# A graph layer on one core: two engines copy a tile of rows in every eighth chunk instead of every sixteenth

## The chip, the cores and the metric

The kernel runs on one core of a Trainium2 chip. The metric is the device time of one execution in microseconds; the median over several runs counts. The core has five engines that each work through a queue of instructions in order: TensorE (PE in the profile, its weight loads PEld), VectorE (DVE), ScalarE (ACT), GpSimd (POOL) and SyncE (SP). SP does nothing but issue transfers; ACT and POOL issue transfers beside their own work. Engines wait for each other, and for transfers, by semaphores.

## The reference, cut to what matters

50000 nodes have 128 features each; 850000 edges (50000 of them loops) have a source, a destination and one of 16 types. A layer adds, for every edge, the source's features times the matrix of the edge's type to the destination, adds the node's own product, and applies relu. There are two such layers; at the end the input is added and each row is normalised.

```python
W = jnp.einsum('rb,bio->rio', w_comp, basis)
seg = dst * N_REL + rel
agg = jax.ops.segment_sum(h[src], seg, num_segments=N_ENT * N_REL)
msg = jnp.einsum('nri,rio->no', agg.reshape(N_ENT, N_REL, -1), W)
h = relu(msg + h @ loop_w + bias)           # twice, with two sets of weights
x = layernorm(x + h)
```

## The kernel before, in words

Each type's matrix is a mix of 8 basis matrices. So the kernel first sums, for each node, its sources' features weighted with each of the 8 coefficients, and multiplies by the 8 basis matrices afterwards, in groups of 512 nodes.

The edges come sorted by destination, with the loops taken out: 800000 of them, in 6250 tiles of 128 edges. Ten tiles (K) make a chunk; there are 625 chunks (C), and a chunk covers about 80 destination nodes. For every tile, 128 rows of features are fetched, one row to a partition, and TensorE multiplies the fetched tile with a matrix `hot` that VectorE makes (the 8 coefficients of every edge at the place of its destination in a window of 30 nodes). VectorE adds the products into a ring in SBUF (lines 1130 on), and a group of 512 nodes that is complete is copied out of the ring by ScalarE (line 915), multiplied by the basis (919), passed through relu (934), turned back and stored.

Nearly all the fetching is done by GpSimd: one indirect transfer for each tile, issued by `gather` (line 270), with the 128 row numbers in a tile `index` that is cast from a packed list for 16 chunks at a time (`indexed`, line 1053). The fetched chunks lie in 4 buffers in the first layer and in 9 in the second; in the order of the program, GpSimd is 2 and 7 chunks ahead of TensorE (FETCH).

A few tiles are fetched in another way. In every sixteenth chunk from EARLY on, tile 9 of the chunk (COPIED) is copied row by row by SP, and in every sixteenth chunk eight chunks apart by ACT: class `Copied`, lines 1172 to 1201. GpSimd skips that tile (line 1250), and TensorE reads the copied tile instead (line 1271). For each such tile `load` (line 1178) fetches 128 offsets from a list AWAY in DRAM into the first partition of the tile itself; `copy` (line 1183) reads sixteen of them into registers (lines 1188 and 1190), takes one (`snap`, line 1191) and issues a transfer of one row of 512 bytes (line 1192). The row of partition 0, where the offsets lie, is copied last. Each of the two copiers has one buffer, and its transfers carry semaphores that the framework deals out in turn from a small set, which SP's and ACT's other transfers use too: a transfer whose semaphore is still owed by an earlier one waits for that.

The order of the work is written out: `later(time, what)` puts a piece of work into a heap by its due time, counted in tiles (10 to a chunk), and the loop over the chunks, which writes TensorE's matmuls, takes from the heap what is due. Rows fall due one by one, evenly over 12 chunks, the last 1.6 chunks ahead of the chunk that needs them (`planned`, line 1197). SP's queue also carries the loads and stores of the groups, of the weights, and of the places in the ring (`offsets`, line 1154); ACT's queue also carries copies and activations. In the first layer the edges of later chunks are prepared along the way (runs, rows_of), with transfers on SP and work on VectorE and ACT.

Of the kernel before, what the change touches and what calls it, by code (L numbers as in the profile page):

```python
# [51 lines left out]
P = 128  # L52
# [4 lines left out]
K = 10  # L57
# [10 lines left out]
PER = 5  # L68
# [4 lines left out]
GATHERS = 4  # L73
J = 4
AHEAD = 16
EACH = 2 * len(WINDOWS)
NEAR = 128
BATCH = 4
# [9 lines left out]
WIDE = 1  # L88
PARTS_OF = ((0, 3), (3, 5))
EPS = 1e-5  # L90
EVERY = 16
COPIED = 9
EARLY = ((27, 35), (19, 27))
LEAD = 2
AT_A_TIME = 16


def divisor(n, most):
# [4 lines left out]
def tile_rgcn_resnorm(  # L103
# [15 lines left out]
    nc = tc.nc  # L119
    N, D = x.shape  # L120
# [3 lines left out]
    C = -(-M // (K * P))  # L124
# [34 lines left out]
    consts = ctx.enter_context(tc.tile_pool(name="consts", bufs=1))  # L159
    col = consts.tile([P, P], F32, name="col")  # L160
    nc.gpsimd.iota(col, pattern=[[1, P]], base=0, channel_multiplier=0, allow_small_or_imprecise_dtypes=True)
    part = consts.tile([P, 1], F32, name="part")
    nc.gpsimd.iota(part, pattern=[[0, 1]], base=0, channel_multiplier=1, allow_small_or_imprecise_dtypes=True)
    ident = consts.tile([P, P], F32, name="ident")
    nc.vector.tensor_scalar(ident, col, part, None, op0=OP.is_equal)

    single = consts.tile([P, 4], F32, name="single")
    eps, apart_by, odd, ones = (single[:, i : i + 1] for i in range(4))
    nc.vector.memset(eps, EPS)

# [12 lines left out]
    def weighed(brief):  # L183


        steps = brief.tile([P, AT - 1], F32, name="steps")
        nc.gpsimd.iota(
            steps, pattern=[[NR, AT - 1]], base=NR, channel_multiplier=0, allow_small_or_imprecise_dtypes=True
        )
        passed = brief.tile([P, AT - 1], F32, name="passed")  # L190
        nc.vector.tensor_scalar(passed, steps, part, None, op0=OP.is_le)
        its_tile = brief.tile([P, 1], F32, name="its_tile")
        nc.vector.tensor_reduce(its_tile, passed, AX.X, OP.add)
        nc.vector.scalar_tensor_tensor(its, its_tile, float(-NR), part, op0=OP.mult, op1=OP.add)
        nc.vector.tensor_scalar(its1, its, 1.0, None, op0=OP.add)
        one_tile = brief.tile([P, AT], F32, name="one_tile")
        nc.vector.tensor_scalar(one_tile, col[:, :AT], its_tile, None, op0=OP.is_equal)
        which = brief.tile([P, PARTS], F32, name="which")
        nc.vector.tensor_scalar(which, col[:, :PARTS], its_tile, None, op0=OP.is_equal)
        again = brief.tile([P, PARTS], F32, name="again")  # L200
        nc.vector.tensor_scalar(again, col[:, PARTS : 2 * PARTS], its_tile, None, op0=OP.is_equal)
        nc.vector.tensor_add(which, which, again)
        for n, (basis, w_comp, loop_w, bias) in enumerate(GIVEN):
            ec = brief.tile([P, NB], F32, name="ec")
            nc.scalar.dma_start(
                ec, bass.AP(tensor=w_comp.tensor, offset=w_comp.offset, ap=[[0, AT], [NB, NR], [1, NB]])
            )
            nc.vector.tensor_tensor(
                each[:, n],
                ec[:, None, :].to_broadcast([P, AT, NB]),  # L210
                one_tile[:, :, None].to_broadcast([P, AT, NB]),
                op=OP.mult,
            )

            column_of = consts.tile([P, 1], F32, name=f"bias_of{n}")
            nc.scalar.dma_start(column_of, bass.AP(tensor=bias.tensor, offset=bias.offset, ap=[[1, P], [1, 1]]))
            BIAS_OF.append(column_of)
            left, mine = ec, brief.tile([P, NB], F32, name="mine")
            for i in range(PARTS):
                short = brief.tile([P, NB], BF16, name=f"short{i}")  # L220
                nc.vector.tensor_copy(short, left)
                if i == 0:
                    nc.vector.tensor_scalar(mine, short, which[:, i : i + 1], None, op0=OP.mult)
                else:
                    nc.vector.scalar_tensor_tensor(
                        mine, short, which[:, i : i + 1], mine, op0=OP.mult, op1=OP.add
                    )
# [333 lines left out]
    def rows_of(j, pool):  # L561
# [12 lines left out]
        keyf, srcf = pair(pool, "real_both", LIVE, LIVE, F32)  # L574
# [6 lines left out]
        def put(of, to):  # L581
# [17 lines left out]
        away = pool.tile([P, LIVE, 2], F32, name="full").bitcast(I32).rearrange("p e w -> p (e w)")[:, :P]  # L599
        of_copied = (COPIED - PER) * P  # L600
        nc.vector.tensor_scalar(
            away[:m], srcf[:m, of_copied : of_copied + P], float(N - 1), float(D), op0=OP.min, op1=OP.mult
        )
        nc.sync.dma_start(AWAY[r0 : r0 + m], away[:m])
        begin = pool.tile([P, len(WINDOWS)], F32, name="begin")
# [110 lines left out]
    def chunked():  # L716
        with (
# [334 lines left out]

            def indexed(n, b, copy):
                first_of, end_of = b * AHEAD * K, min(C, (b + 1) * AHEAD) * K
                index[n, b] = hp.tile([P, AHEAD * K], I32, name="index", bufs=3)
                return copy(index[n, b][:, : end_of - first_of], src[:, first_of:end_of])

            placed = indexed(0, 0, nc.vector.tensor_copy)
# [14 lines left out]
            def later_rows():  # L1073
# [12 lines left out]

            coming = later_rows()
            copiers = [
                (engine, [engine.alloc_register(f"copied{who}_{i}") for i in range(AT_A_TIME)])
                for who, engine in enumerate((nc.sync, nc.scalar))  # L1090
            ]
            ordered = ExitStack()
# [1 line left out]
            for n, of in enumerate((x, H1)):  # L1094
# [19 lines left out]
                def places(c):  # L1114
                    loaded_for[0] = n, c // BATCH
                    some = min(BATCH, C - c) * EACH
                    which_of = c % AHEAD // BATCH * BATCH * EACH
                    nc.vector.load(at_reg[:some], offs[c // AHEAD][0:1, which_of : which_of + some])

                def add(c, half, i, pa):  # L1120

# [30 lines left out]
                offs = {}  # L1152

                def offsets(b):
                    first_of, end_of = b * AHEAD * EACH, min(C, (b + 1) * AHEAD) * EACH
                    offs[b] = hp.tile([1, AHEAD * EACH], I32, name="offs")
# [10 lines left out]
                def go_on(now):  # L1167
                    while events and events[0][0] <= now:
                        _, _, what, args = heapq.heappop(events)
                        what(*args)  # L1170

                class Copied:
                    def __init__(self, c, who):
                        self.c, self.who = c, who
                        self.engine, self.at = copiers[who]
                        self.order = [*range(1, P), 0]

                    def load(self):
                        self.to = hp.tile([P, D], F32, name=f"copied{self.who}", bufs=1)
                        self.away = self.to.bitcast(I32)[0:1, :]  # L1180
                        nc.sync.dma_start(self.away, AWAY[2 * self.c + 1 : 2 * self.c + 2])

                    def copy(self, i):
                        p = self.order[i]
                        if i % AT_A_TIME == 0:
                            some = self.order[i : i + AT_A_TIME]
                            if some[-1] == 0:
                                self.engine.load(self.at[AT_A_TIME - 1 :], self.away[:, 0:1])
                                some = some[:-1]
                            self.engine.load(self.at[: len(some)], self.away[:, some[0] : some[-1] + 1])  # L1190
                        at = self.engine.snap(self.at[i % AT_A_TIME], min_val=0, max_val=(N - 1) * D)
                        self.engine.dma_start(
                            self.to[p : p + 1, :],
                            of.rearrange("n d -> (n d)")[ds(at, D)].rearrange("(o d) -> o d", o=1),
                        )

                    def planned(self, queue):
                        begin = K * (self.c - EVERY + LEAD) + PER
                        queue(begin - K, self.load)
                        for i in range(P):  # L1200
                            queue(begin + i * (EVERY - 2 * LEAD) * K // P, self.copy, i)

                copied_rows = {
                    c: Copied(c, who) for who, early in enumerate(EARLY[n]) for c in range(early, C, EVERY)
# [4 lines left out]
                batches = [Weights(c, n) for c in range(0, C, BATCH)]  # L1209
                batches[0].load()  # L1210
                offsets(0)
                for b in range(1, -(-C // AHEAD)):
                    later(K * AHEAD * b - K, offsets, b)
                if n == 0:
                    batches[0].compare()
                    batches[0].multiply()
# [21 lines left out]
                for c in range(C):  # L1238
# [19 lines left out]
                    for half in range(2):  # L1258
# [6 lines left out]
                        for at in range(PER):  # L1265
                            if at < len(tiles):
# [2 lines left out]
                                w, before = WINDOWS[i], NB * sum(WINDOWS[:i])  # L1269
                                fetched = g[:, half * PER + j, :]  # L1270
                                if half * PER + j == COPIED and c in copied_rows:
                                    fetched = copied_rows[c].to
                                nc.tensor.matmul(  # L1273
                                    pa[:, before : before + NB * w],
                                    fetched,
# [234 lines left out]
```

## Time and profile before

| | |
|---|---|
| runs | 15531.8 us median of 3 (15528.1 to 15533.5) |
| profiled execution | 15567.6 us, its span 15565.8 us |
| busy, PE / DVE / ACT / POOL | 62% / 50% / 11% / 75% of the span |
| TensorE clock granted | 0.794 |
| moved by DMA | 1531 MB, 98 GB/s |
| tiles fetched by GpSimd / by SP and ACT | 12349 / 151 |

The profile is of one execution and its engines are abbreviated as above; a q behind an engine's name means its sequencer, which issues transfers and waits. "L270" is line 270 of the kernel. In groups of instructions, the columns are line, engine, operation, output and input, count, then busy us and mean ns of one, then the idle time of the engine before them and what ended it ("issue" is idle time in which nothing that the profile shows was waited for). Lists of waits give the waiting engine and instruction, what it waited for, the total in us, how often and the longest. Issuing a transfer, register work and waiting don't count as busy.

### The profile page before, as it was taken

How to read it: one execution, taken by the hardware profiler on the slowest of the kernel's cores; microseconds unless marked ns; L12 is line 12 of the kernel's file. 1: busy time of each engine (PE TensorE's matmuls, PEld its weight loads, DVE VectorE, ACT ScalarE, POOL GpSimd, SP SyncE). 2: the span in 40 equal slices, each digit the busy share in tenths (PEclk: the TensorE clock that was granted, in tenths of full speed). 3: DMA queues.
4: the chain of work that ended last, by engine and by line, in shares of the span. 5: the costliest groups of instructions: out<-in, count | busy, mean ns of one | idle time of the engine just before them, and what ended most of it. 6: DMA issues, size and time to landing. Idle time of an engine off the chain costs nothing.

```text
span 15565.8 us, 164019 instructions
## 1 busy us (share of the span) xinstructions
PE 9727.8 (62%) x31567; PEld 7176.4 (46%) x31567; DVE 7738.2 (50%) x11079; ACT 1642.8 (11%) x2031; POOL 11742.7 (75%) x12390
## 2 busy tenths in 40 slices
PE   5666566666666666666666666666666666666666
PEld 4444444444444444444444444444444444444444
DVE  7655555565444444444444444444444444444444
ACT  1111111111111111111100000000000000000000
POOL 7777777777777777777777777777777777777777
PEclk7877887777888888888877777787777777777778
DMA  4333333333333333333333333333333333333332
GB/s 125 109 111 107 109 110 106 107 106 105 99 99 96 99 99 98 98 99 98 94 92 94 94 94 94 93 92 93 94 94 94 94 94 94 92 94 94 94 94 81
DMA packets 827507, 1530.93 MB, mean 98 GB/s; under 512 B 245150, under 2 KB 332937, under 8 KB 826472
## 3 DMA queue, kind: packets, MB, share of 16 engines
q0 software_dynamic: 397104, 817.16, 18.8%
q1 hardware_dynamic: 408424, 697.64, 13.4%
q10 hardware_dynamic: 20944, 5.55, 0.2%
q14 instruction: 778, 6.37, 0.1%
q8 instruction: 257, 4.21, 0.1%
HBM read 1391.28 MB, written 128.09 MB: 98 GB/s over the span
## 4 chain that ended last, share of the span: by engine, by line
POOL 61%; issue 24%; DMA 11%; PE 2%; DVE 1%; SPq 1%; ACTq 0%; ACT 0%; POOLq 0%; DVEq 0%
POOL g L270 43%; DMA g<-in_x_dram,index 5%; POOL d_r L270 4%; POOL k_loop L270 4%; POOL parts L270 4%; POOL full L270 4%; POOL real_both L270 3%; DMA g<-H,index 2%; PE pa L1273 1%; DMA real_both<-H,index 1%; DMA full<-H,index 1%; DMA k_loop<-H,index 1%; DMA parts<-H,index 1%; DMA d_r<-H,index 1%; SPq L1190 0%
## 5 line engine op out<-in xcount | busy, mean ns | idle before, releaser
L1273 PE MATMUL pa<-hot,g 128*128 128x240 f32 x17882 | 5490.0, 459 | 4012.8 <-DMA g<-in_x_dram,index 2195.9
L270 POOL DMA_INDIRECT g<-in_x_dram,index x6175 | 5875.3, 951 | 1890.1 <-issue 1783.7
L1273 PEld LDWEIGHTS pa<-hot,g 128*128 128x128 f32 x17882 | 4155.0, 242 | 5580.4 <-issue 2374.8
L1130 DVE TENSOR_TENSOR ring<-pa,ring 128x240 f32 x5000 | 2038.6, 408 | 7077.2 <-PE pa L1273 6275.3
L1106 DVE TENSOR_TENSOR hot<-pm,fixed 128x2400 f32<-128x2400 f32 x1250 | 3317.9, 2654 | 69.7 <-ACT pm L789 17.4
L270 POOL DMA_INDIRECT g<-H,index x2766 | 2616.6, 946 | 857.1 <-issue 814.1
L919 PE MATMUL pn<-own,basis 128*128 128x512 f32 x3072 | 1808.1, 674 | 0.0
L900 DVE TENSOR_TENSOR ring<-wide,pa 128x2048 f32<-128x2048 f32 (+1 forms) x386 | 876.4, 2270 | 230.8 <-DMA wide<-CW 212.2
L915 ACT COPY own<-ring 128x4096 f32<-128x4096 f32 x192 | 692.3, 3606 | 2444.1 <-DVE ring L1130 1100.6
L270 POOL DMA_INDIRECT k_loop<-H,index x682 | 645.2, 946 | 208.1 <-issue 197.4
L270 POOL DMA_INDIRECT real_both<-H,index x682 | 645.3, 946 | 208.0 <-issue 194.3
L270 POOL DMA_INDIRECT d_r<-H,index x682 | 645.2, 946 | 208.0 <-issue 198.6
L270 POOL DMA_INDIRECT parts<-H,index x681 | 644.3, 946 | 207.8 <-issue 197.4
L270 POOL DMA_INDIRECT full<-H,index x681 | 644.2, 946 | 207.8 <-issue 194.7
L919 PEld LDWEIGHTS pn<-own,basis 128*128 128x128 f32 x3072 | 667.3, 219 | 65.5
L1273 PE MATMUL pa<-hot,real_both 128*128 128x240 f32 x1364 | 445.4, 482 | 334.7 <-DMA real_both<-H,index 317.0
L1273 PE MATMUL pa<-hot,k_loop 128*128 128x240 f32 x1364 | 442.6, 479 | 318.7 <-DMA k_loop<-H,index 287.3
L1273 PE MATMUL pa<-hot,full 128*128 128x240 f32 x1362 | 444.3, 481 | 310.5 <-DMA full<-H,index 292.3
L1273 PE MATMUL pa<-hot,d_r 128*128 128x240 f32 x1364 | 442.6, 479 | 311.7 <-DMA d_r<-H,index 275.2
L1273 PE MATMUL pa<-hot,parts 128*128 128x240 f32 x1362 | 444.4, 481 | 304.1 <-DMA parts<-H,index 268.6
L887 ACT COPY pa<-hT 128x512 f32<-128x512 f32 x392 | 228.8, 587 | 3534.0 <-DMA copied<-H 1798.0
L1099 DVE TENSOR_TENSOR fixed<-fixed,key 128x300 f32<-128x300 f32 x1250 | 584.5, 468 | 1.6
(181 smaller groups left out, 5255.8 us busy)
## 6 DMA issues: line engine op xcount, KB each, us to landing
wide<-CW SPq DMA_DIRECT2D x388, 1024.0 KB
g<-in_x_dram,index POOLq DMA_INDIRECT x6175
copied<-in_x_dram SPq DMA_DIRECT2D x4864, 0.5 KB
copied<-H SPq DMA_DIRECT2D x4864, 0.5 KB
copied<-H ACTq DMA_DIRECT2D x4864, 0.5 KB
copied<-in_x_dram ACTq DMA_DIRECT2D x4736, 0.5 KB
rows<-in_x_dram SPq DMA_DIRECT2D x194, 256.0 KB
g<-H,index POOLq DMA_INDIRECT x2766
```

What stands on the lines that cost most here:

```text
L270: return nc.gpsimd.indirect_dma_start(out=to, out_offset=None, in_=of, in_offset=bass.IndirectOffsetOnAxis(ap=idx, axis=0))
L887: nc.scalar.copy(self.laid[b][:, : self.cnt], self.hT[:, : self.cnt])
L900: nc.vector.tensor_tensor(into, wide, laid[:, None, :].to_broadcast([P, AT_ONCE, cnt]), op=OP.mult)
L915: nc.scalar.copy(self.sums, ring[:, :, at : at + cnt])
L919: nc.tensor.matmul(self.pn[:, a:e], BASIS[:, b, :], self.sums[:, b, a:e], start=False, stop=b == NB - 1)
L1099: nc.vector.tensor_tensor(own, grid[:, None, :].to_broadcast([P, K, WN]), key[:, c * K : (c + 1) * K, None].to_broadcast([P, K, WN]), op=O ...
L1106: nc.vector.tensor_tensor(hot, pm[:, c % BATCH * K * NB : (c % BATCH + 1) * K * NB].rearrange("e (k b) -> e k b", b=NB)[:, :, :, None].to_ ...
L1130: nc.vector.tensor_tensor(into, pa[:, before : before + NB * w].rearrange("d (b w) -> d b w", w=w), into, op=OP.add,)
L1273: nc.tensor.matmul(pa[:, before : before + NB * w], fetched, hot[:, half * PER + j].rearrange("e b w -> e (b w)"), start=(i, j) == mine[i][0],
```

## The change

The copiers take a tile in every eighth chunk each. The due times move: a tile's rows are spread over 8 chunks, and the last is due 0.6 chunk ahead of its chunk. Each copier has two buffers and four semaphores of its own, one for a tile in turn; the rows carry that semaphore and no other, and TensorE waits for it before it reads the tile. The offsets in AWAY are kept in bytes, the rows are addressed as bytes, and the register is used without `snap`. The offsets lie in the last partition of the tile, so rows go in the order 0 to 127. To make room in SBUF, `index` has two buffers and not three, the places in the ring are fetched for 8 chunks at a time, two chunks ahead (they were fetched for 16, one ahead), and some single columns share a tile.

```diff
+PLACED = 8
-EVERY = 16
+EVERY = 8
 COPIED = 9
-EARLY = ((27, 35), (19, 27))
+EARLY = ((20, 24), (12, 16))
 LEAD = 2
 AT_A_TIME = 16
+SIGNALS = 4
+DONE = 16
...
-            away[:m], srcf[:m, of_copied : of_copied + P], float(N - 1), float(D), op0=OP.min, op1=OP.mult
+            away[:m], srcf[:m, of_copied : of_copied + P], float(N - 1), float(4 * D), op0=OP.min, op1=OP.mult
...
-                index[n, b] = hp.tile([P, AHEAD * K], I32, name="index", bufs=3)
+                index[n, b] = hp.tile([P, AHEAD * K], I32, name="index")
...
-                (engine, [engine.alloc_register(f"copied{who}_{i}") for i in range(AT_A_TIME)])
+                (
+                    engine,
+                    [engine.alloc_register(f"copied{who}_{i}") for i in range(AT_A_TIME)],
+                    [tc.alloc_semaphore(f"rows{who}_{i}") for i in range(SIGNALS)],
+                    [0],
+                )
...
-                    which_of = c % AHEAD // BATCH * BATCH * EACH
-                    nc.vector.load(at_reg[:some], offs[c // AHEAD][0:1, which_of : which_of + some])
+                    which_of = c % PLACED // BATCH * BATCH * EACH
+                    nc.vector.load(at_reg[:some], offs[c // PLACED][0:1, which_of : which_of + some])
...
+                bytes_of = of.rearrange("n d -> (n d)").bitcast(U8)
+
                 class Copied:
                     def __init__(self, c, who):
                         self.c, self.who = c, who
-                        self.engine, self.at = copiers[who]
-                        self.order = [*range(1, P), 0]
+                        self.engine, self.at, signals, used = copiers[who]
+                        self.signal = signals[used[0] % SIGNALS]
+                        self.after = (used[0] // SIGNALS + 1) * P * DONE
+                        used[0] += 1
+                        self.group = f"copied{n}_{c}"
 
                     def load(self):
-                        self.to = hp.tile([P, D], F32, name=f"copied{self.who}", bufs=1)
-                        self.away = self.to.bitcast(I32)[0:1, :]
+                        self.to = hp.tile([P, D], F32, name=f"copied{self.who}")
+                        self.away = self.to.bitcast(I32)[P - 1 : P, :]
+                        self.rows = self.to.bitcast(U8)
                         nc.sync.dma_start(self.away, AWAY[2 * self.c + 1 : 2 * self.c + 2])
 
-                    def copy(self, i):
-                        p = self.order[i]
-                        if i % AT_A_TIME == 0:
-                            some = self.order[i : i + AT_A_TIME]
-                            if some[-1] == 0:
-                                self.engine.load(self.at[AT_A_TIME - 1 :], self.away[:, 0:1])
-                                some = some[:-1]
-                            self.engine.load(self.at[: len(some)], self.away[:, some[0] : some[-1] + 1])
-                        at = self.engine.snap(self.at[i % AT_A_TIME], min_val=0, max_val=(N - 1) * D)
-                        self.engine.dma_start(
-                            self.to[p : p + 1, :],
-                            of.rearrange("n d -> (n d)")[ds(at, D)].rearrange("(o d) -> o d", o=1),
+                    def copy(self, p):
+                        if p % AT_A_TIME == 0:
+                            self.engine.load(self.at, self.away[:, p : p + AT_A_TIME])
+                        at = RuntimeValue.of_register_unchecked(
+                            self.at[p % AT_A_TIME], min_val=0, max_val=(N - 1) * 4 * D
                         )
+                        row = self.engine.dma_start(
+                            self.rows[p : p + 1, :], bytes_of[ds(at, 4 * D)].rearrange("(o d) -> o d", o=1)
+                        )
+                        row.then_inc(self.signal, DONE)
+                        tc.no_tile_sem_insts.add(row.ins.name)
+                        tc.add_to_no_dep_group(self.group, row.ins)
+
+                    def landed(self):
+                        tc.declare_fence(nc.tensor.wait_ge(self.signal, self.after).ins, group=self.group)
+                        return self.to
 
                     def planned(self, queue):
-                        begin = K * (self.c - EVERY + LEAD) + PER
+                        begin = K * (self.c - EVERY - LEAD + 1) + PER
                         queue(begin - K, self.load)
                         for i in range(P):
-                            queue(begin + i * (EVERY - 2 * LEAD) * K // P, self.copy, i)
+                            queue(begin + i * EVERY * K // P, self.copy, i)
...
-                for b in range(1, -(-C // AHEAD)):
-                    later(K * AHEAD * b - K, offsets, b)
+                for b in range(1, -(-C // PLACED)):
+                    later(K * PLACED * b - 2 * K, offsets, b)
...
-                                    fetched = copied_rows[c].to
+                                    fetched = copied_rows[c].landed()
```

More of the change, by code (lines that the diff above doesn't have):

```diff
@@ L38 @@
 from concourse._compat import with_exitstack
-from concourse.bass import ds
+from concourse.bass import RuntimeValue, ds
 F32 = mybir.dt.float32
@@ L161, in tile_rgcn_resnorm @@
     nc.gpsimd.iota(col, pattern=[[1, P]], base=0, channel_multiplier=0, allow_small_or_imprecise_dtypes=True)
-    part = consts.tile([P, 1], F32, name="part")
+    single = consts.tile([P, 8], F32, name="single")
+    part = single[:, 4:5]
     nc.gpsimd.iota(part, pattern=[[0, 1]], base=0, channel_multiplier=1, allow_small_or_imprecise_dtypes=True)
@@ L165, in tile_rgcn_resnorm @@
     nc.vector.tensor_scalar(ident, col, part, None, op0=OP.is_equal)
-    single = consts.tile([P, 4], F32, name="single")
     eps, apart_by, odd, ones = (single[:, i : i + 1] for i in range(4))
@@ L213, in weighed @@
             )
-            column_of = consts.tile([P, 1], F32, name=f"bias_of{n}")
+            column_of = single[:, 5 + n : 6 + n]
             nc.scalar.dma_start(column_of, bass.AP(tensor=bias.tensor, offset=bias.offset, ap=[[1, P], [1, 1]]))
@@ L1154, in offsets @@
                 def offsets(b):
-                    first_of, end_of = b * AHEAD * EACH, min(C, (b + 1) * AHEAD) * EACH
-                    offs[b] = hp.tile([1, AHEAD * EACH], I32, name="offs")
+                    first_of, end_of = b * PLACED * EACH, min(C, (b + 1) * PLACED) * EACH
+                    offs[b] = hp.tile([1, PLACED * EACH], I32, name="offs")
                     nc.sync.dma_start(
```

## The prediction

> **What bounds the kernel now.** I read the page first: busy times, slices, chain of waits.
>
> ```profile
> span 15565.8 us, 164019 instructions
> PE 9727.8 (62%) x31567; PEld 7176.4 (46%) x31567; DVE 7738.2 (50%) x11079; ACT 1642.8 (11%) x2031; POOL 11742.7 (75%) x12390
> ...
> POOL 7777777777777777777777777777777777777777
> ...
> DMA  4333333333333333333333333333333333333332
> ...
> POOL 61%; issue 24%; DMA 11%; PE 2%; DVE 1%; SPq 1%; ACTq 0%; ACT 0%; POOLq 0%; DVEq 0%
> ```
>
> POOL is the busiest engine, evenly in all forty slices. Its 75% hide a gap after each gather, so the groups of L270, the one line that issues gathers, come next (columns: count, busy us and mean ns, idle us before them).
>
> ```profile
> L270 POOL DMA_INDIRECT g<-in_x_dram,index x6175 | 5875.3, 951 | 1890.1 <-issue 1783.7
> ...
> L270 POOL DMA_INDIRECT g<-H,index x2766 | 2616.6, 946 | 857.1 <-issue 814.1
> ...
> L270 POOL DMA_INDIRECT k_loop<-H,index x682 | 645.2, 946 | 208.1 <-issue 197.4
> L270 POOL DMA_INDIRECT real_both<-H,index x682 | 645.3, 946 | 208.0 <-issue 194.3
> L270 POOL DMA_INDIRECT d_r<-H,index x682 | 645.2, 946 | 208.0 <-issue 198.6
> L270 POOL DMA_INDIRECT parts<-H,index x681 | 644.3, 946 | 207.8 <-issue 197.4
> L270 POOL DMA_INDIRECT full<-H,index x681 | 644.2, 946 | 207.8 <-issue 194.7
> ```
>
> The counts add to 12349 gathers, busy to 11716 us, idle to 3787 us: together 15503 of the 15566 us span. All but 63 us is gather after gather. The windows view of L270 alone, in a stretch of each layer (columns: length, busy, count, granted clock, DMA share, GB/s), gives the pitch:
>
> ```profile
> 4000.00:5000.00 1000.00, 756.20 (x800) 0.82 0.33 97
> 9000.00:10000.00 1000.00, 756.17 (x800) 0.79 0.31 95
> ```
>
> 800 in 1000 us is 1.25 us each, about 0.95 busy and 0.30 fixed gap. Whether another engine holds POOL back is read from POOL's waits (total us, times, longest):
>
> ```profile
> POOL g L270 <- issue: 2597.8, 8476, 13.7
> ...
> POOL g L270 <- DMA g<-in_x_dram,index: 75.7, 248, 0.3
> ...
> POOL g L270 <- PE pa L1273: 11.9, 39, 0.3
> ```
>
> None of its waits for data or buffers exceeds 0.3 us, the usual gap: buffers are free in time. The time is the number of gathers times 1.25 us.
>
> **The change: what leaves POOL.** A tile that SyncE (SP) or ScalarE (ACT) copies is a gather that POOL doesn't issue. Now there are 38+37 such tiles in the first layer (chunks 27, 43, ... and 35, 51, ... of 625) and 38+38 in the second: 151, and indeed 12500 − 12349 = 151. With every eighth chunk from 20, 24 and from 12, 16 there are 76+76 and 77+77: 306. So 155 gathers go, and 155 × 1.25 = 193.8 us (by the mean of all gathers, 15503/12349 = 1.255, 194.6).
>
> **What SP and ACT get.** The view of the tile `copied` (ns min/median/max):
>
> ```profile
> L1192 SPq DMA_DIRECT2D copied<-in_x_dram x4864: 224/228/922, 123.5 to 7688.8; - x195
> ...
> L1192 ACTq MOVE copied<-H x4864: 29/29/29, 7932.4 to 15442.3; - x195
> L1192 ACTq DMA_DIRECT2D copied<-H x4864: 224/225/540, 7932.5 to 15442.4; - x195
> ...
> L1190 SPq TENSOR_LOAD <-copied x608: 3257/3524/5519, 119.4 to 15326.6; - x152
> L1190 ACTq TENSOR_LOAD <-copied x600: 3212/3738/6103, 304.4 to 15425.0; - x150
> ...
> L1181 SPq DMA_DIRECT2D copied<-AWAY x151: 215/231/867, 110.2 to 15287.0; - x151
> ...
> L1188 ACTq TENSOR_LOAD <-copied x75: 470/570/702, 431.3 to 15424.3; - x75
> ```
>
> And the timelines, ACT's first, then two of SP's (start, length, first issue to end of last):
>
> ```profile
> 6007.54 2.17 ACTq L1192 DMA_DIRECT2D copied<-in_x_dram  x6
> 6009.75 0.57 ACT L869 COPY lrel<-pa 16x512 f32<-16x512 f32 x1 [1.28 <-DMA copied<-in_x_dram]
> 6009.89 17.26 ACTq L1192 DMA_DIRECT2D copied<-in_x_dram  x13
> ```
> ```profile
> 6010.86 1.46 SPq L1192 DMA_DIRECT2D copied<-in_x_dram  x4
> ```
> ```profile
> 9000.46 0.35 SPq L817 DMA_DIRECT2D hT<-H1T  x1
> 9000.91 0.38 SPq L964 DMA_DIRECT2D out_dram<-t  x1
> ...
> 9004.69 0.40 SPq L874 DMA_DIRECT2D wide<-CW  x1
> ```
>
> Unhindered, a row costs (2.17 − 0.22)/5 = 0.39 us on ACT and (1.46 − 0.23)/3 = 0.41 us on SP, of which 0.224 is the issue itself. The 13 rows in 17.26 us contain 5.0 us of rows and two register loads of 0.57 and 3.74: the other 8 us are waits inside the row train, which today takes semaphores shared with other transfers. Semaphores per tile remove those. Byte addresses and the dropped `snap` remove register steps; the new pitch isn't shown, so I bound it: at most today's 0.39 to 0.41, at least the bare 0.224. I take 0.32, since one of the two steps (the 29 ns MOVE and the snap, each with its gap) probably stays.
>
> Per 8 chunks POOL will need 78 × 1.25 = 97.5 us, and each copier has one tile in it:
> - ACT: 8 loads × 3.74 = 29.9; 128 rows × 0.32 = 41 (28.7 to 49.9); its own work 1642.8/15565.8 × 97.5 = 10.3, counted in full though the 869 copy above still runs when the next row is issued. Sum 81, at most 90.
> - SP: 8 × 3.52 = 28.2; rows 41 (to 52.5); its other transfers at 0.35 to 0.40 each. I allow 20 in 97.5 us, 8 us, the doubled fetches of AWAY (0.23 each) and of the offsets included. Sum 77, at most 89.
>
> Both fit under 97.5, so the copying hides behind POOL's gathers and costs nothing there; if that cover went, each us over would be paid in each of 156 periods. What queues behind a row on ACT is every activation and copy (line 887's feeds VectorE, 789's the weights), on SP every load.
>
> **Waits moved.** TensorE gets a wait for the tile's semaphore (`landed`), with all later matmuls behind it. The last row falls due 0.6 chunk (of 12.5 us) ahead of the chunk, now 1.6. A late TensorE touches POOL only when a gather finds its buffer in use, some 3 chunks in the first layer (4 buffers) and 8 in the second (9): 37 and 100 us. Zero in the sum; the upper bound is the second rival. The second buffer removes SP's largest wait (columns as above):
>
> ```profile
> SPq L1181 <- PE pa L1273: 1812.3, 142, 27.7
> ...
> SPq L824 <- DMA LREL<-l_rel,l_to: 139.8, 7, 34.8
> ...
> SPq L568 <- DMA FULL<-full,to_i: 67.5, 5, 34.3
> ```
>
> It was off POOL's path, so nothing is gained by it. Index tiles with two buffers in place of three are rewritten 13 chunks after their last use, the offsets are fetched two chunks ahead: zero for both, covered by those chunks. New too: ACT's tile serves the last chunk, 624, of each layer, where no later gather hides lateness. At worst a load and sixteen rows, 3.7 + 16 × 0.39 = 10 us in each layer; I take 1 us each, since the row train ends 0.6 chunk before.
>
> **Sum**, against the profiled execution (15567.6 us): 15567.6 − 193.8 + 2 = 15375.8. The median of the runs is 35.8 us under it, so 15340.
>
> **Rivals.**
> 1. *ACT becomes the bound (slower).* ACT works in order, and waits inside its queue stop rows too.
>
> ```profile
> ACT sd L702 <- DVE mv L700: 1226.1, 68, 26.4
> ACT own L915 <- DVE ring L1130: 1100.6, 80, 82.5
> ACT oT L934 <- PE pn L919: 1020.7, 69, 51.3
> ...
> ACT pa L887 <- DVE ring L1130: 913.4, 82, 23.1
> ```
>
> These four are 4261 us, 27.4% of the span, 26.7 us in a period. At the upper 90 us of service only 7.5 us are free: from 28% of these waits left over, ACT decides. With 40%, 10.7 us, a period is 100.7 and 156.25 of them 15730 us. For it: the load doubles and the waits are long. Against: they are those of an engine that arrived early, and a busier ACT arrives later; at the middle pitch 60% would have to stay. 0.10.
> 2. *Rows late in the first layer.* While the edges are prepared SP is held for up to 34.8 us at once (lines 824 and 568, 207 us in total); added to rows due 12.5 us later than now, that passes the 37 us of slack. If half of the held time reaches POOL, 104 us of the gain go: 15445. Against: the slack is measured from TensorE, which waits for data now. 0.09.
> 3. *Nothing gained.* POOL's pitch would have to grow by 16 ns, 193.8 us over 12194 gathers, under twice the row traffic. The two layers differ by 5 ns (951 and 946) and the pitch is the same in both; the copying was on throughout. 15530; 0.04.
> 4. *One DMA engine fills up.* The queue whose 5.55 MB are ACT's 9600 rows of 0.5 KB and little else (packets, MB, share) shows
>
> ```profile
> q10 hardware_dynamic: 20944, 5.55, 0.2%
> ```
>
> 0.2% (0.25 at most) of 16 engines' span is at most 623 us for 9600 rows, 65 ns each. If one engine took all 39168 rows, that is 2.5 ms, 17% of it, beside a mean share of 0.33. For it to decide, a row would need 0.67 × 97.5/256 = 255 ns; at 300 ns the period is 76.8 + 32.2 = 109 us, 17030 us. 0.02.
> The Trainium skill (DMA: Bandwidth & Descriptors, on why a DMA increments its semaphore by 16) has the rule behind this one: a transfer from SP or ACT runs on as many of the sixteen engines, from the lowest-numbered up, as divide its slowest dimension, so one-row copies would all pile up on one. By it the sum stays as it is up to the row price above. No row here shows the engines apart.
>
> **How the numbers follow.** The forecast, 15340, has 0.75, with an own range of 15320 (pitch mean in place of 1.25, no loss at the ends, and the runs' spread) to 15390 (both ends at worst, 20 us, and some late rows). With the second rival's 0.09 the range 15320 to 15470 holds a little over 8 in 10. Under 0.2%, 31 us, a measurement of this kernel can't tell a change from none. Faster: 0.75 + 0.09 = 0.84. Same: the third rival and edges of others, 0.05. Slower: 0.11.
>
> **What will show it.** 12194 gathers at L270; the pitch 1.25 in the middle windows still; `copied` with 39168 rows; row trains of 0.22 to 0.39 us without gaps; POOL's waits on PE still at 0.3 us. I'd be wrong if POOL's waits name PE for tens of us, if TensorE waits for `copied` by the chunk, or if ACT's slices show no wait left, its row trains unbroken from tile to tile.

## The result, and the profile after

The changed kernel takes 15374.0 us (median; 15372.0 to 15376.3), the kernel before 15532.7: a ratio of 0.9898 (95% interval 0.9881 to 0.9916), 158.7 us less. The forecast was 15340, its range 15320 to 15470. So the direction, the mechanism and the range held, and 34 us of the gain are missing. Every run below has its own runs of the kernel before beside it, 15541 us for the first four and 15532 for the next four; for the last four it took 20196 us, so these four are compared with nothing outside their set.

The page after: span, engines, chain.

```profile
span 15374.4 us, 185496 instructions
...
PE 9626.2 (63%) x31567; PEld 7126.1 (46%) x31567; DVE 7738.6 (50%) x11079; ACT 1653.7 (11%) x2031; POOL 11563.1 (75%) x12235
...
POOL 63%; issue 26%; DMA 7%; PE 2%; DVE 1%; ACTq 0%; ACT 0%; SPq 0%; DVEq 0%; POOLq 0%
```

POOL is still the bound. The groups of the gathers (L273 is the old L270):

```profile
L273 POOL DMA_INDIRECT g<-in_x_dram,index x6098 | 5782.8, 948 | 1868.4 <-issue 1796.5
...
L273 POOL DMA_INDIRECT g<-H,index x2731 | 2577.3, 944 | 878.5 <-issue 814.8
L273 POOL DMA_INDIRECT parts<-H,index x673 | 635.3, 944 | 205.3 <-issue 200.4
```

With the four other row buffers, at x673 each, that is 6098 + 2731 + 5 × 673 = 12194 gathers: 155 fewer, as counted. The two middle windows of L273 (length, busy, count, clock, DMA share, GB/s):

```profile
4000.00:5000.00 1000.00, 755.60 (x802) 0.81 0.36 100
9000.00:10000.00 1000.00, 755.81 (x801) 0.79 0.33 94
```

The pitch is 1.247 to 1.248 us: twice the row traffic hasn't slowed the gathers. What the copiers spend is in the view of the tile `copied` (ns min/median/max), and a row train of ACT and one of SP in the timelines:

```profile
L1203 ACTq DMA_DIRECT2D copied<-H x9856: 227/228/547, 7750.1 to 15329.0; - x198
...
L1199 SPq TENSOR_LOAD <-copied x1224: 1183/1282/3644, 118.7 to 15270.9; - x175
L1199 ACTq TENSOR_LOAD <-copied x1224: 1224/1339/2616, 232.1 to 15322.2; - x175
```
```profile
6013.11 1.51 ACTq L1203 DMA_DIRECT2D copied<-in_x_dram  x5
```
```profile
6078.13 2.85 SPq L1203 DMA_DIRECT2D copied<-in_x_dram  x9
```

A row costs (1.51 − 0.23)/4 = 0.32 us on ACT and (2.85 − 0.23)/8 = 0.33 on SP, the value taken in the forecast. A register load fell from 3.5 and 3.7 us to 1.28 and 1.34, which was not forecast. ACT's sum for a period of 97.5 us is then 8 × 1.34 + 128 × 0.32 + 10.3 = 62 us, not 81.

Where the 34 us went is in POOL's waits:

```profile
POOL g L273 <- DMA H<-t: 45.7, 1, 45.7
...
POOL g L273 <- PE pa L1290: 9.8, 32, 0.3
```

A single wait of 45.7 us stands there: the first gather of the second layer, which reads H, the first layer's output, and waits for its last rows. The timelines around it, POOL before the change, then POOL and ACT after:

```profile
7805.57 0.95 POOL L270 DMA_INDIRECT g<-in_x_dram,index  x1 [0.30 <-issue]
7820.17 0.95 POOL L270 DMA_INDIRECT g<-H,index  x1 [13.65 <-issue]
```
```profile
7682.09 0.94 POOL L273 DMA_INDIRECT g<-in_x_dram,index  x1 [2.31 <-ACT index L1059]
...
7692.07 0.94 POOL L273 DMA_INDIRECT g<-in_x_dram,index  x1 [0.30 <-issue]
7738.69 0.94 POOL L273 DMA_INDIRECT g<-H,index  x1 [45.69 <-DMA H<-t]
```
```profile
7612.32 0.86 ACTq L1203 DMA_DIRECT2D copied<-in_x_dram  x3
7681.62 0.20 ACT L1059 CAST index<-src 128x10 int32<-128x10 uint16 x1 [68.79 <-DMA g<-in_x_dram,index]
7681.69 14.09 ACTq L1203 DMA_DIRECT2D copied<-in_x_dram  x34
7695.91 0.69 ACT L937 ACTIVATE oT<-pn,single 128x512 f32<-128x512 f32 x1 [14.09 <-issue]
```

From the last gather of the first layer to the first of the second it took 14.60 us before and takes 46.62 now, 32.0 more; the last chunk's gathers also waited 2.31 − 0.30 = 2.0 us for an index. Together 34.0. ACT shows the reason: it stood 68.8 us in front of the cast at line 1059 of the index for chunk 624, waiting for gathers, and behind that cast were 34 rows of its tile for chunk 624 and the activations of the last groups.

### The profile page after: what moved, and what is told of

Read it like the earlier page. It is cut to its first block, busy times and chain, and to the rows that moved or that the text cites. A ratio compares the mean times of both kernels' runs of the same rounds, so it can differ in the third digit from the quotient of the medians.

```text
span 15374.4 us, 185496 instructions
## 1 busy us (share of the span) xinstructions
PE 9626.2 (63%) x31567; PEld 7126.1 (46%) x31567; DVE 7738.6 (50%) x11079; ACT 1653.7 (11%) x2031; POOL 11563.1 (75%) x12235
## 3 DMA queue, kind: packets, MB, share of 16 engines
q1 hardware_dynamic: 428602, 702.80, 13.9%
q10 hardware_dynamic: 40912, 10.70, 0.4%
## 4 chain that ended last, share of the span: by engine, by line
POOL 63%; issue 26%; DMA 7%; PE 2%; DVE 1%; ACTq 0%; ACT 0%; SPq 0%; DVEq 0%; POOLq 0%
POOL g L273 45%; DMA g<-in_x_dram,index 4%; POOL d_r L273 4%; POOL real_both L273 4%; POOL full L273 4%; POOL parts L273 4%; POOL k_loop L273 4%; PE pa L1290 1%; DMA g<-H,index 1%; PE pn L922 0%; DMA k_loop<-H,index 0%; DMA full<-H,index 0%; DMA parts<-H,index 0%; PE pa L780 0%; DMA real_both<-H,index 0%
## 5 line engine op out<-in xcount | busy, mean ns | idle before, releaser
L1290 PE MATMUL pa<-hot,g 128*128 128x240 f32 x17658 | 5417.1, 458 | 3945.9 <-DMA g<-in_x_dram,index 2292.6
L273 POOL DMA_INDIRECT g<-in_x_dram,index x6098 | 5782.8, 948 | 1868.4 <-issue 1796.5
L1290 PEld LDWEIGHTS pa<-hot,g 128*128 128x128 f32 x17658 | 4097.3, 242 | 5484.3 <-issue 2571.6
L273 POOL DMA_INDIRECT g<-H,index x2731 | 2577.3, 944 | 878.5 <-issue 814.8
L273 POOL DMA_INDIRECT parts<-H,index x673 | 635.3, 944 | 205.3 <-issue 200.4
L273 POOL DMA_INDIRECT k_loop<-H,index x673 | 635.2, 944 | 205.4 <-issue 201.1
L273 POOL DMA_INDIRECT full<-H,index x673 | 635.1, 944 | 205.4 <-issue 199.6
L273 POOL DMA_INDIRECT d_r<-H,index x673 | 635.1, 944 | 205.3 <-issue 201.1
L273 POOL DMA_INDIRECT real_both<-H,index x673 | 635.0, 944 | 205.3 <-issue 200.7
L1290 PEld LDWEIGHTS pa<-hot,real_both 128*128 128x128 f32 x1346 | 331.8, 255 | 456.9 <-issue 185.4
```

Source lines behind the costliest of these rows:

```text
L273: return nc.gpsimd.indirect_dma_start(out=to, out_offset=None, in_=of, in_offset=bass.IndirectOffsetOnAxis(ap=idx, axis=0))
L1290: nc.tensor.matmul(pa[:, before : before + NB * w], fetched, hot[:, half * PER + j].rearrange("e b w -> e (b w)"), start=(i, j) == mine[i][0],
```

## The experiments

Theory: two index tiles are one too few at one place. Index tiles are cast in the order: chunks 608 to 623, then the first of the second layer (at chunk 617, early), then chunk 624. With two buffers the third of these waits until the first is read, that is for the gathers of chunk 623. The rivals: ACT's copied tile in the last chunk is to blame by itself, or the missing time is spread as a slower pitch.

**The cast moved**

```diff
-                    if n == 0 and c == C - AHEAD // 2:
+                    if n == 0 and c == C - 1:
                         indexed(1, 0, nc.scalar.copy)
```

> The changed kernel with one edit: the cast of the second layer's first index tile moves from chunk 617 to the last chunk, 624, of the first layer. In the changed kernel ACT stood 68.8 us in front of the cast for chunk 624 (line 1059), and the first gather of the second layer came 45.7 us late, against 12.7 to 14.6 before. Theory A (two index tiles are too few where three are alive, so that this cast waits for the gathers of chunk 623): ACT doesn't stop, the stall at the layer's end falls back to 15 us or so, the time falls by 30 to 35 us to 15340. Rival B (the stall comes from ACT's copied tile in the last chunk alone): the tile is still there, so nothing changes, 15374. Rival C (35 us are spread over the layers as a slower pitch of the gathers): 15374.

Measured: 15351.2 us (15350.3 to 15355.2) beside 15541.1 for the kernel before, a ratio of 0.9878 (0.9862 to 0.9895), 189.9 us less in place of 158.7. POOL's wait, and ACT at the cast for chunk 624 and at the moved one:

```profile
POOL g L273 <- DMA H<-t: 13.9, 1, 13.9
```
```profile
7615.73 0.20 ACT L1059 CAST index<-src 128x10 int32<-128x10 uint16 x1 [0.68 <-issue]
7615.81 14.19 ACTq L1203 DMA_DIRECT2D copied<-in_x_dram  x34
...
7685.22 0.32 ACT L1059 CAST index<-src 128x160 int32<-128x160 uint16 x1 [22.73 <-DMA g<-in_x_dram,index]
```

The cast for chunk 624 no longer waits, the 34 rows go out 66 us earlier, and the stall is back at 13.9 us. The second layer's cast waits now, but nothing urgent is behind it. Rivals B and C fall: the copied tile is still in chunk 624, and 31 of the 34 us came back. Beside the kernel before, 190 of the forecast 192 us (193.8 − 2) are there.

**No copied tile in the last chunk, the early cast left in**

```diff
-                    c: Copied(c, who) for who, early in enumerate(EARLY[n]) for c in range(early, C, EVERY)
+                    c: Copied(c, who) for who, early in enumerate(EARLY[n]) for c in range(early, C - 1, EVERY)
```

> The changed kernel, but ACT copies no tile in chunk 624, the last of each layer; GpSimd gathers these two tiles (12196 gathers in place of 12194, 2.5 us more). The early cast stays. Theory A (the cast holds ACT): ACT still waits about 69 us for the cast, but 34 rows of 0.39 us, 14 us, no longer stand between the cast and the activation at line 937; the stall falls from 46 to some 32 us, the time to 15363. Rival B (the copied tile alone): the stall falls to 15 us, the time to 15345.

Measured: 15364.1 us (15358.3 to 15369.1) beside the same 15541.1, 177.0 us less. The wait of POOL and ACT's cast:

```profile
POOL g L273 <- DMA H<-t: 27.0, 1, 27.0
```
```profile
7682.46 0.20 ACT L1059 CAST index<-src 128x10 int32<-128x10 uint16 x1 [71.69 <-DMA g<-in_x_dram,index]
7682.57 0.69 ACT L937 ACTIVATE oT<-pn,single 128x512 f32<-128x512 f32 x1
```

ACT waits just as long, and the activation follows at once. So the stall has two parts: 13 us (27.0 − 13.9) from the held activations and 19 us (45.7 − 27.0) from the rows of the last tile that stood between, 14 us of issuing and what followed.

**The kernel before with two index tiles**

```diff
-                index[n, b] = hp.tile([P, AHEAD * K], I32, name="index", bufs=3)
+                index[n, b] = hp.tile([P, AHEAD * K], I32, name="index")
```

> The kernel before with one part of the change: index has two buffers and not three. Theory A: at the end of the first layer ACT waits for the gathers of chunk 623 before the cast for chunk 624, GpSimd waits some 2 us for that cast, and the activations behind it come late; without rows behind the cast the stall at the layer's end grows from 14.6 to about 30 us; 15548, 0.1% slower, and the wait of some 60 to 70 us shows at the cast. Rival B: no change, 15533.

Measured: 15554.9 us (15546.3 to 15559.5) beside 15541.1, a ratio of 1.0009 (1.0000 to 1.0019): 14 us slower, at the edge of what can be told. ACT, POOL's first gather of the second layer, then POOL's gathers in two windows:

```profile
7775.04 0.20 ACT L1056 CAST index<-src 128x10 int32<-128x10 uint16 x1 [72.11 <-DMA g<-in_x_dram,index]
7775.15 0.69 ACT L934 ACTIVATE oT<-pn,bias_of 128x512 f32<-128x512 f32 x1
```
```profile
7813.81 0.94 POOL L270 DMA_INDIRECT g<-H,index  x1 [26.12 <-issue]
```
```profile
4000.00:5000.00 1000.00, 755.81 (x802) 0.81 0.35 98
9000.00:10000.00 1000.00, 755.76 (x802) 0.78 0.33 94
```

The same wait of 72 us, without any of the change's copying, and the stall grows from 13.65 to 26.1 us. The 13 us of the run before this one agree. The windows bear on a smaller point: with this one edit the kernel before gathers at 802 in 1000 us. The 800 of its first profile, 0.25% of 15500 us or 39 us, is about what that execution (15567.6 us) lay above the median, so it most likely belongs to that execution and not to the kernel; no second trace of the unedited kernel shows it.

**Shared semaphores again (with the moved cast)**

```diff
-                        row = self.engine.dma_start(
+                        self.engine.dma_start(
                             self.rows[p : p + 1, :], bytes_of[ds(at, 4 * D)].rearrange("(o d) -> o d", o=1)
                         )
-                        row.then_inc(self.signal, DONE)
-                        tc.no_tile_sem_insts.add(row.ins.name)
-                        tc.add_to_no_dep_group(self.group, row.ins)
...
-                        tc.declare_fence(nc.tensor.wait_ge(self.signal, self.after).ins, group=self.group)
                         return self.to
```

> The kernel with the late cast (first run of this set), but the rows carry the framework's shared semaphores again; byte addresses, two buffers and every eighth chunk stay. In the kernel before, 13 rows and two loads took 17.3 us where 9.3 us are work, some 0.6 us of waiting for each row. Theory A (the copiers need their own semaphores to keep up): 128 x (0.32 + 0.6) + 8 x 1.3 = 128 us of ACT in a period of 97.5: ACT sets the pace, and the time is far over the kernel before, 18000 us or more. Rival (those waits stood only where a copier was early, and shrink when it is busy): no change against the late cast, 15340.

Measured: 15351.4 us (15349.7 to 15353.3), a ratio of 0.9877 (0.9861 to 0.9894), the same as the moved cast with its own semaphores. SP's waits:

```profile
SPq L1203 <- DMA copied<-H: 1680.7, 1541, 11.0
SPq L1203 <- DMA copied<-in_x_dram: 1618.6, 1653, 11.8
```

3300 us of waiting inside SP's row trains, and not a microsecond of it reaches the end. Theory A falls clearly. At every eighth chunk the semaphores per tile are worth nothing: the waits, 21.6 us of SP for each of its 153 tiles, lie in the 35 us of a period in which a copier has nothing else to do.

**What made the register loads fast**

Two runs, both with the moved cast. In the first, a load starts at a column that is one over a multiple of sixteen, from the last partition; in the second, at a multiple of sixteen, from the first partition.

```diff
+                        self.order = [*range(1, P - 1), 0, P - 1]
...
-                    def copy(self, p):
-                        if p % AT_A_TIME == 0:
-                            self.engine.load(self.at, self.away[:, p : p + AT_A_TIME])
+                    def copy(self, i):
+                        p = self.order[i]
+                        if i % AT_A_TIME == 0:
+                            if i < P - AT_A_TIME:
+                                self.engine.load(self.at, self.away[:, p : p + AT_A_TIME])
...
```

> The late-cast kernel; offsets stay in the last partition, but a register load reads sixteen of them from column 1 mod 16 on, as the kernel before does (rows 1 to 126, then 0 and 127). A load of sixteen took 3.5 us on SP and 3.7 on ACT before, and 1.28 and 1.34 in the changed kernel. Theory A (the first column decides): 3.5 us again. Theory B (the partition, 0 or 127, decides): 1.3 us. The time of the kernel stays within 10 us either way, since 8 x 3.7 + 41 + 10 us of ACT fit in the period of 97.5.

```diff
+                        self.order = [*range(AT_A_TIME, P), *range(1, AT_A_TIME), 0]
...
-                        self.away = self.to.bitcast(I32)[P - 1 : P, :]
+                        self.away = self.to.bitcast(I32)[0:1, :]
...
+                        if i % AT_A_TIME == 0:
+                            first_of = i + AT_A_TIME if i < P - AT_A_TIME else 0
+                            self.engine.load(self.at, self.away[:, first_of : first_of + AT_A_TIME])
```

> The late-cast kernel; offsets lie in the first partition, as before the change, but every register load starts at a multiple of sixteen columns. Theory A (the first column decides): 1.3 us for a load. Theory B (the partition decides): 3.5 us.

Measured, in the same order, from the view of the tile:

```profile
L1202 SPq TENSOR_LOAD <-copied x1071: 3637/3737/6121, 119.3 to 15232.5; - x179
L1202 ACTq TENSOR_LOAD <-copied x1071: 3760/3878/7130, 233.6 to 15278.2; - x179
```
```profile
L1202 SPq TENSOR_LOAD <-copied x1224: 1132/1232/3302, 119.7 to 15235.1; - x175
L1202 ACTq TENSOR_LOAD <-copied x1224: 1179/1299/2611, 234.5 to 15287.7; - x175
```

The first column decides; the first and the last partition give the same. The change got it as a side effect: with the offsets in the last partition, rows go from 0 to 127 and each load starts at a multiple of sixteen. The times are 15345.3 and 15341.2 us (one run each) beside 15532.1: three times the load time costs nothing that can be told, since 8 × 3.88 + 41 + 10.3 = 82 us fit in 97.5.

**More copied tiles: every sixth and every fifth chunk (with the moved cast)**

```diff
-EVERY = 8
+EVERY = 6
...
-EARLY = ((20, 24), (12, 16))
+EARLY = ((20, 23), (12, 15))
```

> The late-cast kernel with a copied tile in every sixth chunk for each copier: 407 tiles, 12093 gathers. Theory (GpSimd's gathers bound the kernel, the copiers have room): 101 gathers fewer x 1.249 = 126 us under the late cast, 15225; ACT's sum is 41 + 10.7 + 7.7 = 59 us in a period of 72.4. Rival (the copiers are already near their limit): the time doesn't fall below 15300, and TensorE waits for the copied tiles.

Measured: 15219.2 us (15217.4 to 15221.5) beside 15532.1, a ratio of 0.9798 (0.9782 to 0.9814). It beats both kernels. The windows of the gathers are untouched:

```profile
4000.00:5000.00 1000.00, 755.67 (x801) 0.80 0.37 101
9000.00:10000.00 1000.00, 755.55 (x802) 0.80 0.34 95
```

For every fifth chunk `EVERY` is 5 and `EARLY` ((20, 22), (12, 14)).

> The same with every fifth chunk: 488 tiles, 12012 gathers. If GpSimd still bounds: 182 gathers fewer than the late cast, 227 us, 15124. ACT's sum is 41 + 10.7 + 6.4 = 58 us in a period of 60, so this is the edge: if waits inside ACT's queue don't shrink under load, ACT decides, a period becomes 65 us or more, and the time goes over 16000.

Measured: 15428.9 us (15427.5 to 15432.9) beside 15532.1, a ratio of 0.9934 (0.9917 to 0.9951): still faster than before, but 210 us slower than with every sixth. Neither number expected came: not 15124, and not over 16000. The windows of the gathers, one in each layer; what TensorE waited for; the engines' shares of the chain that ended last; and SP's timeline in the first layer:

```profile
4000.00:5000.00 1000.00, 731.69 (x776) 0.80 0.39 99
9000.00:10000.00 1000.00, 752.00 (x797) 0.79 0.38 96
```
```profile
PE pa L1290 <- ACT pm L792: 815.7, 84, 22.8
...
PE pa L1290 <- PEq L1211: 641.2, 111, 17.5
```
```profile
POOL 31%; DMA 21%; issue 18%; SPq 18%; ACTq 5%; PE 3%; DVE 3%; ACT 0%; DVEq 0%; PEld 0%; POOLq 0%; PEldq 0%
```
```profile
4036.39 18.47 SPq L1203 DMA_DIRECT2D copied<-in_x_dram  x41
4054.91 0.64 SPq L758 DMA_DIRECT2D rel<-REL  x1
4055.60 0.45 SPq L798 DMA_DIRECT2D PM<-pm  x1
4056.18 3.96 SPq L1203 DMA_DIRECT2D copied<-in_x_dram  x8
```

The copier that has no time left is SP, in the first layer: its trains of rows and its other transfers follow each other almost without a gap. In the window from 4000 to 5000 us all of SP's waits add to 26 us; they were 183 us with every sixth chunk and 366 us in the changed kernel. So SP is at work for 974 us of the 1000, which is 60 us in each 61.9 us that 48 gathers take at this rate, and at GpSimd's own pitch those 48 take 59.9 us. In the same window SP's rows and register loads (L1203, L1199) hold 34.4% and 10.4% of the chain, ACT's 8.7% and 2.8%, and the fetch of offsets from AWAY, which SP does for both copiers, 6.5%. TensorE is then late at the copied tiles (L1211 is its wait for the tile's semaphore) and at the weights that ACT copies between its rows (L792), and POOL falls to 776 gathers in 1000 us. In the second layer, from 9000 to 10000 us, SP still has 57 us of waits and POOL does 797; whether the nine buffers help there was not shown. This is the first rival's mechanism, but on SP and not on ACT. The sum expected before the run, 58 of 60 us, was ACT's, and it left out the queue that was fuller. All this is read from the trace; no run with less work for SP alone was made.

**Four runs in which the copiers themselves were slow**

Every sixth chunk with shared semaphores; every sixth with loads off the multiple of sixteen; every sixth in the first layer and fifth in the second; every fourth (each with the edits above).

> The late-cast kernel with every sixth chunk, but the rows carry the shared semaphores. At every eighth chunk shared and own semaphores took the same time (15351 both), with 3300 us of waits at SP's rows. With every sixth chunk a period is 72.4 us. Theory A (waits for shared semaphores shrink when a copier is busy): 15219, as with its own. Theory B (they cost a busy copier a fixed time, at SP 3300/153 = 21.6 us a tile): SP's sum is 41 + 10.3 + 6 + 21.6 = 79 us, over 72.4: the time goes to 15500 or more.

> The late-cast kernel with every sixth chunk and its own semaphores, but the register loads start at column 1 mod 16 and take 3.7 to 3.9 us each in place of 1.3. ACT's sum is 41 + 31 + 7.7 = 80 us in a period of 72.4; without its activations, which run beside the rows, 72. Theory (a copier's sum against the period decides, and the aligned offsets are what made room): ACT becomes the bound, 15400 to 16500. Rival (the copiers aren't near a limit): 15219.

> The late-cast kernel with every sixth chunk in the first layer and every fifth in the second: 448 tiles, 12052 gathers, 41 fewer than with six in both. With five in both, the gathers of the second layer ran nearly at full pace (796 to 797 in 1000 us) and those of the first did not (764 to 776). If the nine buffers of the second layer cover the copiers' lateness wholly: 51 us less, 15168. If the second layer loses what it lost with five (796.5 against 801 in 1000 us, 0.55% of 7500 us, 41 us): 15209.

> Every fourth chunk: 610 tiles, 11890 gathers. Bounded by gathers it would take 15219 - 203 x 1.249 = 14966. The period is 38 x 1.249 = 47.5 us, and ACT needs 41 + 10.7 = 52 us, 57 with its activations: ACT sets the pace, 312.5 x 52 to 57 = 16200 to 17800.

Measured: 24006.6, 25247.9, 23724.3 and 27603.3 us, beside 20196.2 for the kernel before. SP in the third of them, a stretch of its timeline, then a row of the tile's view:

```profile
9009.73 12.25 SPq L1203 DMA_DIRECT2D copied<-in_x_dram  x7
9022.08 0.32 SPq L873 DMA_DIRECT2D CW<-lrel  x1
9022.49 3.83 SPq L1203 DMA_DIRECT2D copied<-in_x_dram  x12
```
```profile
L1203 SPq MOVE copied<-H x15744: 1/29/1480, 11376.2 to 23679.9; - x200
```

Seven rows take 12.25 us, then twelve take 3.83: for stretches, SP went forward at a fraction of its rate. The waits on record don't explain it: SP's add to under 5 us from 9000 to 10000 us, and even a register move, 29 ns in the median, took up to 1480 ns. POOL's waits in this run name TensorE:

```profile
POOL g L273 <- PE pa L1290: 4429.6, 349, 41.0
```

None of the expected numbers can be held against these, so three questions stay open: whether a busier copier needs its own semaphores, whether the aligned loads are what makes room at every sixth chunk, and whether five in the second layer alone would pay. The granted clock was lower too, 0.66 to 0.68 in these four and 0.70 in the kernel before beside them, against 0.79 to 0.81 in the other runs. What the runs do show is that all four, which copy more tiles than the kernel before, were 17 to 37% slower than it here. That slow copiers are the whole reason is not shown: no trace of the kernel before was taken beside them.

## Why the prediction was right, and where it was off

- *POOL bounds, 155 gathers go, 1.25 us each.* Right: 12194 gathers, pitch 1.248, 193.4 us; with the cast moved, 190 us show in the time. One reading was too strong: not every wait of POOL stayed at 0.3 us. A single one for VectorE (`POOL g L270 <- DVE turns L611`) takes 7.9 us, and 7.8 after the change, and the longest in the first row shown, 13.7 us, is the stall between the layers. The change made just this stall longer.
- *The copiers fit.* Right, with more room than taken: the row's 0.32 us was met, the load's 3.74 us was 1.34, and TensorE's waits list none for a copied tile's semaphore. That the change's new semaphores would take the waits out of the row trains was right as well, but the trains didn't need it at this rate.
- *Index tiles with two buffers: zero, covered by 13 chunks.* This is the step that failed. It looked at two successive tiles within a layer. At the end of the first layer a third is alive, the second layer's, cast early; ACT then waits for chunk 623's gathers with the last tile's rows and activations behind it. It cost 34 us, shown by moving one cast (31 us back), by taking the last copied tile away (about 18 of them back), and by the kernel before, which loses 14 us from two index tiles alone.
- *Lateness at the layers' ends, 1 us each, 10 at most.* For the first layer its bound was too low, since it counted ACT's own row train and not what ACT might be held by. At the second layer's end there is no early cast, and the size was right: from the start of the last gather to the end of the span it took 22.7 us before and 24.0 now.
- *Rival 1* did not happen at every eighth chunk, but the four waits listed for it, 4261 us, did not shrink there either: the same four rows add to 7642 us after the change, and to 1244 us at every fifth chunk. They are no clean measure of a queue's free time, since they also count time in which ACT's queue issues rows: after the change, a wait of 4.71 us for TensorE that ends at 6005 us covers a train of nine rows that takes 4.41 us. What the rival feared, a copier whose work fills the period, came at every fifth chunk, and on SP, whose sum the prediction had put below ACT's (77 against 81 us). *Rival 2*: POOL's waits on TensorE stayed at 0.3 us each, so rows weren't late enough to matter in the first layer. *Rival 3*: the pitch didn't grow. *Rival 4* got no support: ACT's queue went from 0.2% to

```profile
q10 hardware_dynamic: 40912, 10.70, 0.4%
```

for 19584 rows, 0.4% of 16 × 15374 us or 50 ns a row, far under the 255 ns that it needed. The queue's 40912 packets are about two for each row, so a row isn't spread over the sixteen engines; that all rows share the same engine, as the prediction took from the Trainium skill (DMA: Bandwidth & Descriptors, on why a DMA increments its semaphore by 16), no run here shows. The Trainium skill's rule there goes by the slowest dimension that isn't of size 1, a condition that the prediction left out.

## What to carry to other kernels

When one engine issues small transfers back to back, the kernel's time is their count times the pitch, and moving a few of them to idle queues pays in full until the busiest copier's own sum (issue, register loads, its other work) reaches the period. Sum up every queue that helps, and look at the waits that it has left: here 366 and 183 us of SP's waits in 1000 us, at every eighth and every sixth chunk, went without loss, and 26 at every fifth did not. Before a buffer is taken away, list the tiles that are alive together at the seams (layer ends, early prefetches), not in the steady state: the wait sits in an in-order queue, and everything behind it is late. A wait inside an engine's queue cost nothing here while the engine had idle time to take it up; what it costs a queue that is full was not shown.

## What the hardware showed that was not expected

A register load of sixteen words from SBUF takes 1.23 to 1.34 us when its first column is a multiple of sixteen words and 3.52 to 3.88 us when it is one further (medians on SP and ACT), from the first partition as from the last; other columns were not tried. The Trainium skill (Runtime: NRT & Kernel Launch, Instruction fetch mechanics) gives about 200 ns for each register, even in bulk, for loads that by its Terms come from HBM. The shifted loads from SBUF come near it, at 3.74/16 = 0.23 us, and the aligned ones do not, at 0.08 us.

In the last four runs SP and ACT advanced for stretches at about a third of their usual rate or less (12.25 us for seven rows), while a gather of POOL still took its 0.94 us. The cause was not found.
